# A scan layer's step size summed by TensorE, with its two PSUM banks held as one tile

## The chip, the cores and the metric

The kernel runs on one core of one Trainium2 chip. The metric is the time of one execution in microseconds (us) of device time. Before the change the median of three runs is 3457.79 us (3455.21 to 3458.74). A profiled execution of the same kernel gives the trace that all rows below come from.

The core has five instruction streams that run beside each other and wait for one another by semaphores: PE (TensorE, matrix products, which write into PSUM), DVE (VectorE), ACT (ScalarE), POOL (GpSimd) and SP, which here only issues DMAs. Each stream is strictly in order: an instruction that waits holds up everything behind it on its engine.

## What is computed

The network has four layers on an input of 3 x 256 x 48 x 48 in fp32: a block with attention, a convolution with mixed kernels, a plain convolution, and a selective scan ("layer 3"). Only the scan layer is touched. Cut to what matters, with x the group-normalised input as a sequence of L = 2304 tokens for each of 3 images:

```python
xn  = layernorm(x)                                   # 256 channels
u   = silu(conv1d(xn @ in_proj_w[:512], 4 taps))     # 512 channels
z   = xn @ in_proj_w[512:]
dt_raw, B, C = split(u @ x_proj_w, (16, 16, 16))
dt  = softplus(dt_raw @ dt_proj_w + dt_proj_b)       # 512 channels
for t in range(L):
    h = h * exp(dt[t] * A) + dt[t] * B[t] * u[t]     # 512 x 16 states
    y[t] = sum_n h * C[t]
out = ((y + u * D) * silu(z)) @ out_proj_w
```

The change concerns the line with softplus. In both kernels it is computed as max(v, 0) + ln(1 + exp(-|v|)), where v is what stands in PSUM after the product with dt_proj_w.

## The kernel before

**Tiles.** The 3 x 2304 tokens are worked through in 18 chunks of 384 (CH). The 512 channels are four groups of 128 partitions (m = 0 to 3). For one chunk and one m the 16 states of 128 channels are handled in two steps (h = 0, 1), so a chunk has eight steps; a step has eight parts, one scan each.

**One step.** `fill` (L1711 on DVE, L1715 on POOL) writes dt\*u\*B for the step into the tile hs. `decay` (L1740, ACT) writes exp(dt\*A) for one part into one of three PSUM slots `ps_da`; the decay for part n+3 is issued right after the scan of part n. `scan` (L1748, DVE) runs the recurrence of one part. After the eight parts `times_c` (L1765, POOL) multiplies by C, `add_states` (L1782, PE) sums the states into `ps_y`, and three steps later `gate` (L1789, DVE) reads `ps_y`. `spread_pe` (L1689, PE) copies rows of dt\*u into `ps_r` for the fill two steps ahead. `spread` (L1681) reads dt and dt\*u back from DRAM by DMA, rearranged, for the decays and POOL's fills.

**The preparation.** While one chunk is scanned, the next one's u, B, C, dt and z are made, and the layer norm of the chunk after that. All of it goes through two PSUM banks, `bank[0]` and `bank[1]` (L1206), each a tile of its own, that every stage uses in turn: `less_mean` and `centre` (layer norm), `square_mean`, `inverse_root`, `normalise`; `taps` and `take_u` (u); `project_u` and `take_dbc` (B, C and dt_raw); `project_dt`, `softplus`, `take_dt`, `keep_dt` (dt, two groups at a time: m0 = 0, then 2); `project_z` and `take_z`; `project_y` and `store` (the layer's output).

**The order.** It is written by hand. `plan`, `after` and `gating` (L1373 to L1420) list the stages with a half step j = 0 to 15 and a place in it. `run` (L1422) issues them from the loop of L1800: MID behind the decay of the second of four parts, DONE behind the third, LATE behind the fourth; PE_ at the end of the half step. `keep_order` (L1849) then fixes, for PE, DVE, ACT and POOL, the order in which the instructions were written. So a stage of the preparation stands in the same queue between two decays or two scans. Semaphores are placed automatically, tile by tile, from what each instruction reads and writes.

Chunk 0 is prepared earlier, in `early_preparation` (L1428), while the plain convolution still runs; there each `yield` hands over to the convolution's next group of products. 17 chunks are prepared inside the scan stage, 16 of them with their layer norm.

Of the kernel before, what the change touches and what calls it, by code (L numbers as in the profile page):

```python
# [9 lines left out]
F32 = mybir.dt.float32  # L10
I32 = mybir.dt.int32
AF = mybir.ActivationFunctionType
ALU = mybir.AluOpType
# [3 lines left out]
P = 128  # L17
# [3 lines left out]
CT = 2  # L21
# [4 lines left out]
CH = 384  # L26
# [57 lines left out]
def net(  # L84
# [21 lines left out]
    nc = tc.nc  # L106
# [18 lines left out]
    ident = const.tile([P, P], F32, name="ident")  # L125
# [254 lines left out]
    with ExitStack() as l0:  # L380
# [36 lines left out]
        with ExitStack() as p1:  # L417
# [15 lines left out]
            for b in ORDER:  # L433
# [23 lines left out]
                for c in range(NCH):  # L457
                    for m, dst in ((0, y1), (1, cur[b])):
                        pm = ps.tile([P, 512], F32, tag="s", name="ps_y")
                        for ct in range(CT):  # L460
                            nc.tensor.matmul(  # L461
                                pm[:, :CH], ws[:, ct, m * P : (m + 1) * P], chunk(xb[:, ct, :], c),
                                start=ct == 0, stop=ct == CT - 1,
# [48 lines left out]
        def hidden(b, c):  # L512
            wf, fb = mlp[b]
            f = fpool.tile([P, 2, CH], F32, name="f")
            pf = pair()
            for m in range(2):
                nc.tensor.matmul(
                    pf[:, m, :CH], wf[:, m * P : (m + 1) * P], chunk(cur[b], c),
                    start=True, stop=True,
                )  # L520
            for m in range(2):
                nc.scalar.activation(f[:, m, :], pf[:, m, :CH], AF.Gelu, bias=fb[:, m : m + 1])
            return f
# [10 lines left out]
        with ExitStack() as p2:  # L534
# [9 lines left out]
            for i in range(NB):  # L544
# [400 lines left out]
                for mt in range(0, NT, 2):  # L945
                    pv = pair()
                    for j in range(2):
                        nc.tensor.matmul(
                            pv[:, j, :384], cur[2][:, (mt + j) * P : (mt + j + 1) * P], wn[2],
                            start=True, stop=True,  # L950
# [21 lines left out]
                if i + 1 < NB:  # L972
# [4 lines left out]
                    for b in ORDER:  # L977
                        for c in range(NCH):
                            f = hidden(b, c)
# [84 lines left out]
        for n, b in enumerate(ORDER):  # L1064
            held = None
            for c in range(NCH):
                f = hidden(b, c)
# [38 lines left out]
    psg = ctx.enter_context(tc.tile_pool(name="psg", bufs=1, space=PSUM))  # L1106
    rooms, w3v, chunks, stored = {}, {}, {}, set()

    def room(k, name):
        return rooms[name][k.at % len(rooms[name])]  # L1110
# [47 lines left out]
    def x2_rooms():  # L1158

        block = xpools[2].tile([P, CT, N], F32, name="x2").rearrange("p a b -> p (a b)")  # L1160

        winx, cwb = (t for _, t in divide(
            block, ("winx", P, (CT, DI * P)), ("cwb", P, (DCONV, DI * P))
        ))
        nc.sync.dma_start(winx, w3x.rearrange("(t p) n -> p t n", p=P))
        for k in range(DCONV):
            nc.sync.dma_start(cwb[:, k, :], convw[k : k + 1, :].broadcast_to([P, DI * P]))
        for name, t in divide(
            block, ("u", P, (DI, CH)), ("dtu", P, (DI, CH)), ("dt", P, (DI, CH))
        ):  # L1170
            rooms[name] = [t]
        return winx, cwb

    def fold_taps(winx, cwb, k):
        nc.vector.tensor_tensor(
            w3v["wtap"][:, k, :, :], winx,
            cwb[:, k, :].unsqueeze(1).broadcast_to([P, CT, DI * P]), ALU.mult,
        )
# [15 lines left out]
    def fetch(at):  # L1194
        k = chunks[at] = Chunk()
        k.at = at
        k.b, k.c = todo[at]
        k.before = chunks.get(at - 1)
        k.xg = room(k, "xg")
        nc.sync.dma_start(k.xg, xd[k.b][:, :, k.c * CH : (k.c + 1) * CH])  # L1200
# [2 lines left out]
        pass  # L1203


    bank = [psg.tile([P, 512], F32, name=f"ps_g{j}")[:, :CH] for j in range(2)]  # L1206

    def group_scale(k):  # L1210
        sc, sh = norm3[k.b]
        for ct in range(CT):
            nc.scalar.activation(
                k.xg[:, ct, :], k.xg[:, ct, :], AF.Identity,
                bias=sh[:, ct : ct + 1], scale=sc[:, ct : ct + 1],
            )

    def less_mean(k):

        for to in range(CT):  # L1220
            for ct in range(CT):
                nc.tensor.matmul(  # L1222
                    bank[to], w3v["less"][:, int(to != ct), :], k.xg[:, ct, :],
                    start=ct == 0, stop=ct == CT - 1,
                )

    def square_mean(k):
        for ct in range(CT):
            nc.tensor.matmul(
                bank[1], mean2, k.sq[:, ct, :], start=ct == 0, stop=ct == CT - 1  # L1230
            )

    def centre(k):
        for ct in range(CT):
            nc.scalar.copy(k.xg[:, ct, :], bank[ct])
        k.sq = room(k, "sq")
        nc.scalar.activation(k.sq, k.xg, AF.Square)

    def inverse_root(k):
        var = bank[1]  # L1240
        nc.scalar.activation(var, var, AF.Ln, bias=epst)
        nc.scalar.activation(var, var, AF.Exp, scale=-0.5)

    def normalise(k):
        rs = bank[1].unsqueeze(1).broadcast_to([P, CT, CH])
        nc.vector.tensor_tensor(k.xg, k.xg, rs, ALU.mult)
# [23 lines left out]
    def take_u(k, m):  # L1270
        if m == 0:
            k.u = room(k, "u")
        nc.scalar.activation(
            k.u[:, m, :], bank[m % 2], AF.Identity, bias=v("conv_b", m)
        )
# [31 lines left out]
    def project_dt(k, m0):  # L1307
        for j in range(2):
            m = m0 + j
            nc.tensor.matmul(  # L1310
                bank[j], w3v["dtsb"][:, m * P : (m + 1) * P], k.dbc[: DTR + 1, :],
                start=True, stop=True,
            )

    def softplus(k, m0):

        both = k.dt[:, m0 : m0 + 2, :]
        for j in range(2):
            nc.scalar.activation(k.dt[:, m0 + j, :], bank[j], AF.Abs)
        nc.scalar.activation(both, both, AF.Exp, scale=-1.0)  # L1320
        nc.scalar.activation(both, both, AF.Ln, bias=1.0)

    def take_dt(k, m0):
        for j in range(2):
            m, pdt = m0 + j, bank[j]
            nc.vector.scalar_tensor_tensor(pdt, pdt, 0.0, k.dt[:, m, :], ALU.max, ALU.add)
            nc.vector.tensor_tensor(k.dtu[:, m, :], pdt, k.u[:, m, :], ALU.mult)

    def keep_dt(k, m0):
        for j in range(2):  # L1330
            nc.scalar.copy(k.dt[:, m0 + j, :], bank[j])  # L1331
        if m0 == 0:
            k.dtd, k.dtud = {}, {}
        d = k.dtd[m0] = dram.tile([P, 2, CH], F32, name=f"dtd{m0}")
        nc.sync.dma_start(d, k.dt[:, m0 : m0 + 2, :])
        d = k.dtud[m0] = dram.tile([P // 2, 2, CH], F32, name=f"dtud{m0}")
        nc.sync.dma_start(d, k.dtu[P // 2 :, m0 : m0 + 2, :])

# [25 lines left out]
    def store(k, mo):  # L1364
# [7 lines left out]
    MID, DONE, LATE, PE_ = range(4)  # L1372
# [17 lines left out]
        (7, PE_, 1, project_u),  # L1390
        (8, LATE, 1, take_dbc),
        (8, PE_, 1, lambda k: project_dt(k, 0)),
        (9, LATE, 1, lambda k: softplus(k, 0)),
        (10, MID, 1, lambda k: take_dt(k, 0)),
        (10, DONE, 1, lambda k: keep_dt(k, 0)),
        (10, PE_, 1, lambda k: project_dt(k, 2)),
        (11, LATE, 1, lambda k: softplus(k, 2)),
        (12, MID, 1, lambda k: take_dt(k, 2)),
        (12, DONE, 1, lambda k: keep_dt(k, 2)),
    ]  # L1400

    after = [
# [25 lines left out]
    def early_preparation():  # L1428

        while (2, 1) not in stored:  # L1430
            yield
        fetch(0)
        winx, cwb = x2_rooms()
        k = chunks[0]
        yield
        while 2 not in norm3:
            yield
        group_scale(k)
        yield
        for tap in (0, 1):  # L1440
            fold_taps(winx, cwb, tap)
        less_mean(k)
        yield
        centre(k)
        yield
        square_mean(k)
        yield
        for tap in (2, 3):
            fold_taps(winx, cwb, tap)
        inverse_root(k)  # L1450
        yield
        normalise(k)
        tokens(k)
        fetch(1)
        yield
        for m in (0, 1):
            taps(k, m, 0, 4)
            yield
        take_u(k, 0)
        take_u(k, 1)  # L1460
        yield
        for m in (2, 3):
            taps(k, m, 0, 4)
            yield
        take_u(k, 2)
        take_u(k, 3)
        nc.scalar.activation(k.u, k.u, AF.Silu)
        yield
        k = chunks[1]
        for stage in (group_scale, less_mean, centre, square_mean, inverse_root, normalise):  # L1470
            stage(k)
            yield
        tokens(k)
        yield

        k = chunks[0]
        while 1 not in norm3 or (1, 1) not in stored:
            yield
        x1_rooms()
        yield  # L1480
        project_u(k)
        yield
        take_dbc(k)
        yield
        for m in (0, 2):
            project_dt(k, m)
            yield
            softplus(k, m)
            yield
            take_dt(k, m)  # L1490
            yield
            keep_dt(k, m)
            yield
        for m in (0, 2):
            for j in range(2):
                project_z(k, m + j, j)
            yield
            for j in range(2):
                take_z(k, m + j, j)
            yield  # L1500
# [155 lines left out]
    with ExitStack() as l3:  # L1656
# [136 lines left out]
        k = chunks[0]  # L1793
# [6 lines left out]
        for s, (at, m, h) in enumerate(steps):  # L1800
            if m == 0 and h == 1 and at + 2 <= last:
                fetch(at + 2)
            for part in range(8):
                j = 4 * m + 2 * h + part // 4
# [31 lines left out]
        k = chunks[last]  # L1836
# [122 lines left out]
```

## Time and profile before

| what | value |
| --- | --- |
| runs, median | 3457.79 us |
| profiled execution | 3459.61 us |
| its span in the trace | 3458.2 us |
| scan stage | from about 2020 us to the end |
| clock granted to TensorE, mean | 0.944 |
| ACT busy, whole span | 2351.8 us |
| POOL busy, whole span | 1430.7 us |

How to read what follows. The page gives the busy time of each engine and the costliest groups (line, engine, operation, out<-in, count; then busy us and mean ns of one; then the idle time ahead of them with what ended it). A window row gives busy us of each engine between two times. A timeline row gives start, length, engine, line, operation and count; several equal instructions in a row are merged, and in square brackets stands the idle time before them with what ended it. The tile name ps_g is the banks of the preparation; x, u, wconv and others are blocks of SBUF that hold several things in turn. An fp32 product of 128x384 shows as two instructions.

### The profile page before, as it was taken

What the parts mean: (1) busy time and instruction counts of PE and PEld (TensorE: products, weight loads), DVE (VectorE), ACT (ScalarE), POOL (GpSimd) and SP (SyncE); (2) the same over time, 40 slices, a digit from 0 to 9 for tenths busy, and PEclk for the clock granted to TensorE, in tenths of its full rate; (3) what the DMA queues carried; (4) which work ended last, traced back from release to release, by engine and by line L of the source; (5) the groups of instructions that cost most, each with busy time, mean ns of one, the idle gap of its engine ahead of it and who ended that gap; (6) DMA issues with size and microseconds to landing.
All of it is one profiled execution on the core that took longest, in us unless ns stands there. A gap on an engine that the chain in (4) does not pass through costs nothing.

```text
span 3458.2 us, 51943 instructions
## 1 busy us (share of the span) xinstructions
PE 3125.3 (90%) x20170; PEld 1499.8 (43%) x20170; DVE 2940.7 (85%) x3234; ACT 2351.8 (68%) x3508; POOL 1430.7 (41%) x385
## 2 busy tenths in 40 slices
PE   7999999999999999879999988888888888888885
PEld 4334343443433335447777743333343443333331
DVE  4799899859899994579965379999999999999998
ACT  3788888748888884422224457777777777777774
POOL 0000000000000001110000059999999999999997
PEclk9999999999999999989999989889999999988987
DMA  4000000010000003746402134445444444444441
GB/s 178 14 8 10 8 10 8 8 42 6 10 6 8 10 8 112 249 170 224 139 21 68 46 97 109 115 100 118 116 105 110 106 107 114 116 117 106 117 111 43
DMA packets 167603, 273.95 MB, mean 79 GB/s; under 512 B 30049, under 2 KB 134561, under 8 KB 165426
## 3 DMA queue, kind: packets, MB, share of 16 engines
q1 hardware_dynamic: 154114, 250.48, 26.9%
q10 hardware_dynamic: 13232, 20.06, 1.8%
q8 instruction: 160, 2.62, 0.3%
q14 instruction: 97, 0.79, 0.1%
HBM read 223.12 MB, written 47.10 MB: 78 GB/s over the span
## 4 chain that ended last, share of the span: by engine, by line
PE 54%; DVE 32%; ACT 8%; DMA 3%; issue 2%; POOL 0%; SPq 0%; DVEq 0%; ACTq 0%; POOLq 0%
DVE hs L1748 21%; PE ps_s L637 16%; PE acc L650 14%; PE ps_c L1513 8%; DVE hs L1711 4%; PE ps_g L1222 2%; PE ps_s L1030 2%; ACT ps_da L1740 2%; PE ps_y L461 2%; PE ps_m L664 1%; DVE u L295 1%; PE ps_m L710 1%; ACT L1278 1%; ACT L228 1%; PE acc L528 1%
## 5 line engine op out<-in xcount | busy, mean ns | idle before, releaser
L1748 DVE TENSOR_TENSOR_SCAN hs<-ps_da,hs 128x385 f32<-128x385 f32 x1152 | 1005.6, 938 | 54.4 <-ACT ps_da L1740 35.6
L641 ACT ACTIVATE pt<-ps_s 128x1024 f32<-128x1024 f32 x972 | 942.4, 1022 | 154.8 <-PE ps_s L637 142.2
L856 DVE TENSOR_TENSOR part<-part,pt 128x2048 f32<-128x2048 f32 x396 | 906.6, 2289 | 41.3 <-ACT pt L641 18.5
L1740 ACT ACTIVATE ps_da<-dtr,u 128x384 f32<-128x384 f32 x1152 | 656.0, 582 | 271.3 <-DVE hs L1748 248.4
L163 POOL TENSOR_TENSOR rstd<-ve,mhalf 128x2 f32<-128x2 f32 (+1 forms) x26 | 16.3, 629 | 1477.0 <-DVE ve L161 1477.0
L637 PE MATMUL ps_s<-q,kt 32*128 32x512 f32 (+1 forms) x4320 | 576.4, 592 | 0.1
L650 PE MATMUL acc<-pt,vt 128*32 128x512 f32 (+1 forms) x4320 | 520.9, 561 | 0.2
L1765 POOL TENSOR_TENSOR hc<-hs,x 128x3072 f32<-128x3072 f32 x72 | 446.3, 6198 | 19.8 <-DVE hs L1748 16.5
L1513 PE MATMUL ps_c<-vt,u 128*128 128x288 f32 x1728 | 433.9, 412 | 21.0 <-DVE u L262 21.0
L1765 POOL TENSOR_TENSOR hc<-hs,bc 128x3072 f32<-128x3072 f32 x71 | 438.8, 6181 | 18.6 <-DVE hs L1748 17.2
L1264 PE MATMUL ps_g<-u 128*128 128x384 f32 x1152 | 387.7, 491 | 8.2 <-ACT sz L1349 3.5
L1513 PEld LDWEIGHTS ps_c<-vt,u 128*128 128x128 f32 x1728 | 331.8, 193 | 117.8 <-issue 19.3
L1264 PEld LDWEIGHTS ps_g<-u 128*128 128x128 f32 x1152 | 214.4, 190 | 180.6 <-ACT ps_da L1740 18.7
L637 PEld LDWEIGHTS ps_s<-q,kt 32*128 32x128 f32 x4320 | 195.3, 183 | 199.1 <-issue 120.2
L1782 PE MATMUL ps_y<-hc,u 128*32 128x384 f32 x2304 | 244.8, 548 | 13.8 <-POOL hc L1765 13.8
L1715 POOL TENSOR_TENSOR hs<-dtur,x 128x1536 f32<-128x1536 f32 x72 | 248.4, 3450 | 6.9 <-DMA dtur<-dtud 6.9
L1715 POOL TENSOR_TENSOR hs<-dtur,bc 128x1536 f32<-128x1536 f32 x72 | 249.5, 3465 | 0.0
L650 PEld LDWEIGHTS acc<-pt,vt 128*32 128x32 f32 x4320 | 94.4, 108 | 353.4 <-issue 326.7
L1310 PE MATMUL ps_g<-wconv,u 17*128 17x384 f32 x144 | 79.2, 684 | 82.8 <-ACT x L1331 82.8
L1782 PEld LDWEIGHTS ps_y<-hc,u 128*32 128x32 f32 x2304 | 64.4, 117 | 172.4 <-issue 151.6
L321 POOL MEMSET xpad<- 128x212 f32 x12 | 5.6, 468 | 313.0 <-ACT xpad L1564 234.5
L1529 ACT COPY cb<-ps_c 128x288 f32<-128x288 f32 x48 | 19.2, 400 | 162.9 <-PE ps_c L1513 145.1
(246 smaller groups left out, 3685.3 us busy)
## 6 DMA issues: line engine op xcount, KB each, us to landing
wconv<-in_we SPq DMA_DIRECT2D x144, 384.0 KB, 4.3
dtr<-dtd SPq DMA_DIRECT2D x288, 192.0 KB, 3.9
dtur<-dtud SPq DMA_DIRECT2D x288, 96.0 KB, 4.2
wconv<-xd SPq DMA_DIRECT2D x36, 384.0 KB, 4.3
x<-bcd SPq DMA_DIRECT2D x72, 192.0 KB, 5.7
dtd<-x SPq DMA_DIRECT2D x36, 384.0 KB, 2.9
bc<-bcd SPq DMA_DIRECT2D x72, 192.0 KB, 6.1
yc<-ycat ACTq DMA_DIRECT2D x18, 576.0 KB, 5.0
```

The source lines that it names most:

```text
L637: nc.tensor.matmul(s[:, j, cols], kt[r, mt * P : (mt + 1) * P], q[r, :n], start=True, stop=True,)
L641: nc.scalar.activation(p[:, h0 : h0 + 2, :], s, AF.Exp)
L650: nc.tensor.matmul(acc[h * HD : (h + 1) * HD, :n], vt[:, mt, g * P + h * HD : g * P + (h + 1) * HD], p[:, h, cols], start=mt == 0, stop=mt ...
L856: ): nc.vector.tensor_tensor(part, first, p, ALU.add)
L1264: nc.tensor.matmul(bank[m % 2], w3v["wtap"][:, tap, ct, m * P : (m + 1) * P], k.xn[:, ct, tap : tap + CH], start=tap == 0 and ct == 0, sto ...
L1513: nc.tensor.matmul(pc[:, :HN], u[:, i, dy, ct, m * P : (m + 1) * P], vt[:, i, ct, dy * TW : dy * TW + HN], start=ct == 0 and dy == 0, stop ...
L1711: nc.vector.tensor_tensor(hs[:, :, 0:2, 1:], k.ps[:, :, :CH].unsqueeze(1).broadcast_to([P, 2, 2, CH]), bb, ALU.mult,)
L1715: nc.gpsimd.tensor_tensor(hs[:, :, 2:4, 1:], k.rows[m][1].unsqueeze(1).broadcast_to([P, 2, 2, CH]), bb, ALU.mult,)
L1740: nc.scalar.activation(slots[n % 3][:, 1 : CH + 1], chunks[at].rows[m][0][:, q, :], AF.Exp, scale=amat[:, col : col + 1],)
L1748: nc.vector.tensor_tensor_scan(b, slots[(8 * s + part) % 3][:, : CH + 1], b, 0.0, ALU.mult, ALU.add)
L1765: nc.gpsimd.tensor_tensor(hc, tiles[s][:, :, :, 1:], cb.broadcast_to([P, 2, 4, CH]), ALU.mult)
L1782: nc.tensor.matmul(k.y_ps[32 * q : 32 * q + 32, :CH], fold, hc[:, g, q, :], start=False, stop=h == 1 and g == 1,)
```

## The change

The two banks become one tile of two banks, and both are read by one instruction wherever that is possible (`centre`, the new `positive_part`, `take_dt`, `keep_dt`). max(v, 0) and |v| are taken by ScalarE straight from PSUM; max(v, 0) goes to the room of the other pair of groups (`pair_of(k, 2 - m0)`). After Exp and Ln, TensorE adds the two parts in PSUM by products with the identity matrix (`sum_dt`). VectorE then only multiplies by u.

```diff
-    bank = [psg.tile([P, 512], F32, name=f"ps_g{j}")[:, :CH] for j in range(2)]
+    banks = psg.tile([P, 2, 512], F32, name="ps_g")[:, :, :CH]
+    bank = [banks[:, j, :] for j in range(2)]
...
     def centre(k):
-        for ct in range(CT):
-            nc.scalar.copy(k.xg[:, ct, :], bank[ct])
+        nc.scalar.copy(k.xg, banks)
...
+    def pair_of(k, m0):
+        return k.dt[:, m0 : m0 + 2, :]
+
+    def positive_part(k, m0):
+        nc.scalar.activation(pair_of(k, m0), banks, AF.Abs)
+        nc.scalar.activation(pair_of(k, 2 - m0), banks, AF.Relu)
+
     def softplus(k, m0):
-        both = k.dt[:, m0 : m0 + 2, :]
-        for j in range(2):
-            nc.scalar.activation(k.dt[:, m0 + j, :], bank[j], AF.Abs)
+        both = pair_of(k, m0)
         nc.scalar.activation(both, both, AF.Exp, scale=-1.0)
         nc.scalar.activation(both, both, AF.Ln, bias=1.0)
 
+    def sum_dt(k, m0):
+        for part in (2 - m0, m0):
+            for j in range(2):
+                nc.tensor.matmul(
+                    bank[j], ident, k.dt[:, part + j, :],
+                    start=part != m0, stop=part == m0,
+                )
+
     def take_dt(k, m0):
-        for j in range(2):
-            m, pdt = m0 + j, bank[j]
-            nc.vector.scalar_tensor_tensor(pdt, pdt, 0.0, k.dt[:, m, :], ALU.max, ALU.add)
-            nc.vector.tensor_tensor(k.dtu[:, m, :], pdt, k.u[:, m, :], ALU.mult)
+        nc.vector.tensor_tensor(
+            k.dtu[:, m0 : m0 + 2, :], banks, k.u[:, m0 : m0 + 2, :], ALU.mult
+        )
 
     def keep_dt(k, m0):
-        for j in range(2):
-            nc.scalar.copy(k.dt[:, m0 + j, :], bank[j])
+        nc.scalar.copy(pair_of(k, m0), banks)
...
+        (9, MID, 1, lambda k: positive_part(k, 0)),
         (9, LATE, 1, lambda k: softplus(k, 0)),
-        (10, MID, 1, lambda k: take_dt(k, 0)),
-        (10, DONE, 1, lambda k: keep_dt(k, 0)),
+        (9, PE_, 1, lambda k: sum_dt(k, 0)),
+        (10, DONE, 1, lambda k: take_dt(k, 0)),
+        (10, LATE, 1, lambda k: keep_dt(k, 0)),
         (10, PE_, 1, lambda k: project_dt(k, 2)),
+        (11, MID, 1, lambda k: positive_part(k, 2)),
         (11, LATE, 1, lambda k: softplus(k, 2)),
-        (12, MID, 1, lambda k: take_dt(k, 2)),
-        (12, DONE, 1, lambda k: keep_dt(k, 2)),
+        (11, PE_, 1, lambda k: sum_dt(k, 2)),
+        (12, DONE, 1, lambda k: take_dt(k, 2)),
+        (12, LATE, 1, lambda k: keep_dt(k, 2)),
```

In `early_preparation` the same stages are called in the same order, with one more `yield` for each pair.

The built programs also differ in the semaphores that stages wait for whose lines the diff does not touch. Read from the two programs, for one chunk:

| stage (engine, place) | before it waits for | after it waits for |
| --- | --- | --- |
| take_u(0) (ACT, 2 MID) | last product of taps(0), bank 0 | last product of taps(1), bank 1 |
| take_u(2) (ACT, 5 MID) | last product of taps(2) | last product of taps(3) |
| take_u(3) (ACT, 6 MID) | last product of taps(3) | last product of project_y(0) |
| store(1) (ACT, 8 MID) | last product of project_y(1) | last product of project_u |
| inverse_root, Ln (ACT, 14 MID) | last product of square_mean | last product of project_z(0) |
| normalise (DVE, 15 MID) | no product | last product of project_z(1) |
| take_z(1) (ACT, 15 MID) | last product of project_z(1) | normalise on DVE |
| taps(0) (PE, 0 PE_) | take_z(2) | take_z(3) |
| taps(2) (PE, 3 PE_) | take_u(0) | take_u(1) |
| project_y(0) (PE, 5 PE_) | take_u(2) | take_u(2) |
| positive_part(2), Relu (ACT, 11 MID) | (no such stage) | the DMA that stores dt of the first pair |

More of the change, by code (lines that the diff above doesn't have):

```diff
@@ L1334, in keep_dt @@
         d = k.dtd[m0] = dram.tile([P, 2, CH], F32, name=f"dtd{m0}")
-        nc.sync.dma_start(d, k.dt[:, m0 : m0 + 2, :])
+        nc.sync.dma_start(d, pair_of(k, m0))
         d = k.dtud[m0] = dram.tile([P // 2, 2, CH], F32, name=f"dtud{m0}")
@@ L1487, in early_preparation @@
             yield
+            positive_part(k, m)
             softplus(k, m)
+            yield
+            sum_dt(k, m)
             yield
```

## The prediction

> **What bounds the kernel now.** I read the page's busy times first, then the costliest groups, then the busy times of one chunk of the scan stage, then the four timelines of that chunk.
>
> ```profile
> PE 3125.3 (90%) x20170; PEld 1499.8 (43%) x20170; DVE 2940.7 (85%) x3234; ACT 2351.8 (68%) x3508; POOL 1430.7 (41%) x385
> ...
> L1748 DVE TENSOR_TENSOR_SCAN hs<-ps_da,hs 128x385 f32<-128x385 f32 x1152 | 1005.6, 938 | 54.4 <-ACT ps_da L1740 35.6
> ```
> PE's 90% is an average over other stages. All that the change touches lies behind about 2020 us, where the scans run.
>
> ```profile
> 2411.20:2489.30 78.10, 66.49 (x280) 30.68 (x280) 75.61 (x86) 60.83 (x113) 76.24 (x18) 0.90 0.47 112
> ```
> The columns are window, length, then PE, PEld, DVE, ACT and POOL busy. In one chunk DVE works 75.6 of 78.1 us. POOL, at 76.2, is as full.
>
> ```profile
> 2435.46 6.91 DVE L1748 TENSOR_TENSOR_SCAN hs<-ps_da,hs 128x385 f32<-128x385 f32 x8
> ...
> 2453.82 6.91 DVE L1748 TENSOR_TENSOR_SCAN hs<-ps_da,hs 128x385 f32<-128x385 f32 x8
> ...
> 2472.19 1.81 DVE L1748 TENSOR_TENSOR_SCAN hs<-ps_da,hs 128x385 f32<-128x385 f32 x2
> 2473.92 0.54 DVE L1326 SCALAR_TENSOR_TENSOR ps_g<-ps_g,x 128x384 f32<-128x384 f32 x1
> 2474.49 0.56 DVE L1327 TENSOR_TENSOR x<-ps_g,x 128x384 f32<-128x384 f32 x1
> 2474.97 0.56 DVE L1326 SCALAR_TENSOR_TENSOR ps_g<-ps_g,x 128x384 f32<-128x384 f32 x1
> 2475.56 0.56 DVE L1327 TENSOR_TENSOR x<-ps_g,x 128x384 f32<-128x384 f32 x1
> 2476.03 5.20 DVE L1748 TENSOR_TENSOR_SCAN hs<-ps_da,hs 128x385 f32<-128x385 f32 x6
> ```
> DVE's timeline has hardly a gap (three of 0.47 to 0.58 us in this chunk). So DVE's chain is the end of the stage: a scan starts every 6.91/8 = 0.864 us, and take_dt's four instructions take 2476.03-2473.92 = 2.11 us. POOL runs steps of 9.55 us back to back through most of the chunk (fills start at 2440.43, 2449.99, 2459.52), so it allows 8 x 9.55 = 76.4 us a chunk. DVE's chunk is 78.6 on average (2174.86 to 3196.33 in the chain of waits, 13 chunks). So DVE may win 2.2 us a chunk, no more; what it loses shows in full.
>
> **What the change removes.** In each of 17 chunks, twice, 2.11 us of DVE give way to one 128x768 multiply with a PSUM operand. Nearest row: normalise (L1246), 128x768 with ps_g, takes 0.93 and starts its successor 0.85 later; half a fill (L1711, 128x1536) is 0.87. So 0.86, bounds 0.85 and 1.0: 1.25 won each time, **2.5 us a chunk**.
>
> **What it adds.** (1) TensorE: 8 products of 128x384 in fp32 a chunk, 0.68 us each (L1355, eight instructions for four products, 2.74): 5.5 on 66.5 busy of 78: no bound by itself. (2) ScalarE: ten 384-wide reads of PSUM (0.475) go, seven 768-wide come (0.844, the Exp and Ln rows): 1.2 us more on 60.8, no bound either. ACT rows with one table set show no reload between Exp, Abs and Ln; I take Relu as free of one too. (3) Waits. Both banks are now one tile, and the two built programs differ in what each reader waits for (listed under the change): an instruction on one bank now waits for the last user of either. ScalarE is in order, and behind the waiting instruction stand the decays (L1740) that each scan needs. Decays are three parts ahead of the scans, so a hold costs DVE what exceeds that lead.
>
> I walk the chunk along the rows of before, each time with earlier stalls already added to both sides; hops between engines cost 0.05 (copy's end to L1222's start).
>
> ```profile
> 2429.16 0.85 ACT L1349 COPY sz<-ps_g 128x384 f32<-128x384 f32 x2
> ...
> 2437.82 0.56 ACT L1273 ACTIVATE x<-ps_g,vec 128x384 f32<-128x384 f32 x1
> 2438.28 1.30 ACT L1740 ACTIVATE ps_da<-dtr,u 128x384 f32<-128x384 f32 x2
> ...
> 2450.93 0.56 ACT L1273 ACTIVATE x<-ps_g,vec 128x384 f32<-128x384 f32 x1
> ```
> ```profile
> 2429.78 10.56 PE L1264 MATMUL ps_g<-u 128*128 128x384 f32 x32 [0.51 <-ACT sz L1349]
> ...
> 2449.97 5.43 PE L1264 MATMUL ps_g<-u 128*128 128x384 f32 x16
> ...
> 2478.07 2.92 PE L1310 MATMUL ps_g<-wconv,u 17*128 17x384 f32 x4 [4.92 <-ACT x L1331]
> ```
>
> A. take_u(0) ran at 2437.82, in the midst of PE's taps. Now it waits for taps(1), which end at 2440.34, and 0.38 later because they wait for both take_z copies. It starts at 2440.77, the next decay 0.46 later, ended at 2441.8. That decay serves part 5 of step 1, due at 2435.46+5x0.864 = 2439.78. **Stall 2.1**, from 1.7 (no later start) to 3.
>
> B. take_u(2) (2450.93) now waits for taps(3). taps(2) waits for take_u(1), 2.1 late: 2443.93; then 5.26, the ps_y work 2.17, taps(3) 5.27 (differences of PE starts): 2456.63. Next decay ends 2457.72; part 1 of step 3 is due at 2453.82+0.86+2.1 = 2456.78. **1.0**, from 0.5 (the 0.47 stall of step 2 absorbs it) to 2.
>
> C. take_u(3) waits for project_y(0), which starts only after take_u(2) (2457.29) and needs 3.31: 2460.6. Next decay ends 2461.69, due 2457.77+4x0.864 = 2461.23. **0.5**, from 0 to 1. D. store(1) waits for project_u, 0.6 after its slot, with 0.37 of lead: **0.25**, from 0 to 0.6.
>
> E. project_dt(0) ends at 2470.58. Abs and Relu (0.78 apart), two decays (0.52), Exp (0.88) and Ln (0.84) end at 2474.96. The last two products of sum_dt take 1.37: 2476.4. take_dt, after three scans, is due at 2472.19+2.59 = 2474.78. **1.65**, from 0.8 (Ln a decay earlier) to 2. Behind sum_dt on PE stand the ps_y products (1.43) and spread_pe (0.85); they end near 2478.7, and gate and fill, which read them, are due after 2481: hidden.
>
> F. take_dt and one scan later (2478.16), a decay, then keep_dt's copy, over at 2479.57. project_dt(2) waits for it and takes 2.93 at the slow clock, to 2482.55; Relu also overwrites what the DMA of dtd0 reads (2.9 to landing, 2482.5). ScalarE stands still there for 1.7 us; Abs, Relu and the next decay end at 2484.8. Meanwhile DVE does four scans, gate (0.45) and fill (1.84) and one scan more, due at 2484.77: **0.1**, without the gate and fill 2.4. dtd0 lands 1.2 later than before and is read by spread some 2 us after that, for decays 10 us later still: hidden.
>
> G. One more decay, Exp and Ln end at 2486.95, two products at 2488.35; take_dt is due two scans after 2484.85, at 2486.58: **1.8**, from 1.0 to 2.4.
>
> H. less_mean starts one scan later, as keep_dt moved from DONE to LATE (2412.05 for 2411.19). inverse_root's Ln now waits for project_z(0): at full clock 2.72 for less_mean, copy and Square, 1.4 for square_mean and 1.38 for project_z give 2419.45 for the Ln that ran at 2418.77. Ln, Exp and take_z (0.58+0.47+0.37) put the decay of part 5 at 2421.5, due 2420.43: 1.1, of which 0.58 stands there already, so 0.5. Then normalise on DVE, due 2422.4, waits for project_z(1) (2422.22 to 2423.8): 1.4. With less_mean at its present 4.54, the first rises to 2.2 and hides the second. **2.1**, from 0.5 to 2.5.
>
> Clock: after 4.92 us of idleness L1310's four took 2.92; at 2469.03, after none, 1.55. The waits before these become about 1 to 2 us each; I charge the slow clock in F and half of it in H. (The Trainium skill, "TensorE: Matmul & The Clock Gate", section "What's actually happening", says that a window of about 3.4 us without work halves the clock; by it the shorter pauses keep the clock, and by my estimate from its rule the sum would lose about 0.2 us a chunk.)
>
> At A the row speaks for itself: ScalarE reads one bank at 2437.82 while PE is writing the other until 2440.34. (The Trainium skill, "PSUM — Partial Sum Buffer", section "PSUM bank collisions raise a hardware error", states that only users of the same bank and quadrant of partitions collide. By it none of the waits of A to D and H is needed, and without them the sum would be near +1.05 us a chunk; but the program issues its waits whether or not the memory needs them.)
>
> **Sum.** 2.1+1.0+0.5+0.25+1.65+0.1+1.8+2.1 = 9.5, less 2.5: **+7.0 us a chunk**; x17 = 119, less 2.1 as the norm stage (H) runs in 16: 117. POOL then waits more and binds nothing. At the end of the convolution stage (PE full, 27.0 of 27 us in 1990 to 2017) chunk 0's sum_dt adds 8 x 0.69 = 5.5 us of PE, between nothing (the first scan waits for dtr, landed 2025.67) and 11 (PE also waiting for Ln): +5. The profiled execution took 3459.61 (span 3458.2, 1.4 around it), 1.8 over the median of the runs. 3459.6+122 = 3581.6, less 1.8: **3580 us.**
>
> **Rivals.**
> 1. *The lead of the decays hides all holds* (faster, 3%). Three slots, gate and fill cover a hold at F; if they did so at every place, DVE gains 2.5 and POOL stops it at 2.2: 3457.8-17x2.2 = 3420. It decides if the eight stalls sum to less than 2.5 us. Against it: A alone holds ScalarE 3 us with 0.92 of lead.
> 2. *Only the longer path to dt costs* (7%), so E, F and G remain: 3.55-2.5 = +1.05 a chunk, +18, +5: 3481. For it: ScalarE idles 17 us a chunk. Against it: the waits stand in the built program.
> 3. *More is late* (12%): slow clock at each new pause (8 products at twice 0.68 instead of once) puts up to 1.4 us each on E and G: near +9.5 a chunk, 3625 to 3640.
> The forecast has 78%, with +4 to +9 a chunk: 3525 to 3620. The range takes in most of rival 3 and the lower bounds of E, G and H: **3515 to 3635.** A measurement of this kernel tells about 0.2% from no change. Faster 0.03, within it 0.01, slower 0.96.
>
> **What would show it.** Right: chunks of 85 to 86 us; DVE's scans waiting on decays at step 1 part 5 and step 3 part 1, and take_dt waiting for sum_dt by 1.5 to 2; take_u(0) ending ScalarE's idleness on L1264's last product; POOL idle 8 us a chunk. Wrong: chunks under 80 us (the holds are hidden), or a stall at a place not listed.

## The result and the profile after

The changed kernel takes 3573.44 us in the median of four runs (3572.78 to 3576.57), against 3458.26 us for the kernel before: ratio 1.0335, 95% interval 1.0317 to 1.0353. It is slower by 115 us. The forecast was 3580 us.

The profiled execution took 3572.99 us, 113.4 more than that of before. Two lines of its page, the busy times and the costliest group, answer to the first two shown above.

```profile
PE 3191.7 (89%) x20458; PEld 1538.9 (43%) x20458; DVE 2910.5 (81%) x3126; ACT 2357.5 (66%) x3454; POOL 1433.8 (40%) x385
...
L1768 DVE TENSOR_TENSOR_SCAN hs<-ps_da,hs 128x385 f32<-128x385 f32 x1152 | 1012.8, 940 | 126.4 <-ACT ps_da L1760 109.0 <-POOL hs L1735 1.6
```

DVE is busy for 30 us less, and the scans have waited 109.0 us for decays where it was 35.6. No engine has become full. The line numbers have moved: the scan is now L1768, the decay L1760, sum_dt L1333, take_dt L1339.

The busy times of 15 whole chunks, from the first taps of one chunk to those of the 15th after it, before:

```profile
2115.01:3293.17 1178.16, 1002.90 (x4201) 461.91 (x4201) 1134.58 (x1276) 921.04 (x1768) 1146.00 (x243) 0.90 0.46 111
```

and after:

```profile
2119.82:3400.07 1280.25, 1061.21 (x4441) 495.44 (x4441) 1110.12 (x1186) 925.71 (x1723) 1149.31 (x243) 0.95 0.42 102
```

A chunk went from 78.54 to 85.35 us. DVE's own work (third busy column) fell by 24.5 us, and its idle time rose from 43.6 to 170.1 us. So +8.43 us of standing less 1.63 us of work is the +6.8 us a chunk. The granted clock rose from 0.90 to 0.95, so TensorE was not slower on the whole; at single places it was (see the last section).

DVE's timeline of one chunk after, its rows that end a stall (the time in brackets, and what ended it):

```profile
2984.77 2.66 DVE L1768 TENSOR_TENSOR_SCAN hs<-ps_da,hs 128x385 f32<-128x385 f32 x3 [2.02 <-ACT ps_da L1760]
...
3000.89 3.51 DVE L1768 TENSOR_TENSOR_SCAN hs<-ps_da,hs 128x385 f32<-128x385 f32 x4 [1.04 <-ACT ps_da L1760]
3005.06 2.66 DVE L1768 TENSOR_TENSOR_SCAN hs<-ps_da,hs 128x385 f32<-128x385 f32 x3 [0.66 <-ACT ps_da L1760]
...
3015.04 2.66 DVE L1768 TENSOR_TENSOR_SCAN hs<-ps_da,hs 128x385 f32<-128x385 f32 x3 [0.17 <-ACT ps_da L1760]
...
3023.42 0.96 DVE L1339 TENSOR_TENSOR x<-ps_g,x 128x768 f32<-128x768 f32 x1 [1.30 <-PE ps_g L1333]
...
3035.46 0.96 DVE L1339 TENSOR_TENSOR x<-ps_g,x 128x768 f32<-128x768 f32 x1 [1.95 <-PE ps_g L1333]
...
3048.27 0.96 DVE L1768 TENSOR_TENSOR_SCAN hs<-ps_da,hs 128x385 f32<-128x385 f32 x1 [1.48 <-ACT ps_da L1760]
3049.94 0.95 DVE L1246 TENSOR_TENSOR wconv<-wconv,ps_g 128x768 f32<-128x768 f32 x1 [0.71 <-PE ps_g L1354]
```

These are the stalls A, B, C, D, E, G and the two of H, in this order. ScalarE's rows of the same chunk show what is behind the first two:

```profile
2983.69 0.58 ACT L1273 ACTIVATE x<-ps_g,vec 128x384 f32<-128x384 f32 x1 [2.86 <-PE ps_g L1264]
...
2999.80 0.58 ACT L1273 ACTIVATE x<-ps_g,vec 128x384 f32<-128x384 f32 x1 [3.75 <-PE ps_g L1264]
```

take_u(0) and take_u(2) stand for 2.86 and 3.75 us until TensorE has written the *other* bank, and the decays stand in the queue behind them.

### The profile page after: what moved, and what is told of

It reads as the page before. It is cut to its first block, busy times and chain, and to the rows that moved or that the text cites. A ratio compares the mean times of both kernels' runs of the same rounds, so it can differ in the third digit from the quotient of the medians.

```text
span 3571.3 us, 52385 instructions
## 1 busy us (share of the span) xinstructions
PE 3191.7 (89%) x20458; PEld 1538.9 (43%) x20458; DVE 2910.5 (81%) x3126; ACT 2357.5 (66%) x3454; POOL 1433.8 (40%) x385
## 4 chain that ended last, share of the span: by engine, by line
PE 71%; DVE 13%; ACT 10%; issue 3%; DMA 2%; POOL 0%; SPq 0%; ACTq 0%; DVEq 0%; POOLq 0%
PE ps_s L637 15%; PE acc L650 13%; PE ps_g L1264 11%; PE ps_c L1533 8%; DVE hs L1768 6%; PE ps_g L1333 4%; ACT ps_da L1760 3%; PE ps_y L1802 2%; DVE u L295 2%; PE ps_g L1284 1%; PE ps_y L461 1%; PE ps_s L1030 1%; PE ps_m L664 1%; PE ps_g L1223 1%; PE ps_g L1310 1%
## 5 line engine op out<-in xcount | busy, mean ns | idle before, releaser
L1768 DVE TENSOR_TENSOR_SCAN hs<-ps_da,hs 128x385 f32<-128x385 f32 x1152 | 1012.8, 940 | 126.4 <-ACT ps_da L1760 109.0
L1760 ACT ACTIVATE ps_da<-dtr,u 128x384 f32<-128x384 f32 x1152 | 647.5, 580 | 219.1 <-DVE hs L1768 208.3
L1264 PE MATMUL ps_g<-u 128*128 128x384 f32 x1152 | 387.9, 492 | 49.7 <-ACT x L1362 14.6
L1802 PE MATMUL ps_y<-hc,u 128*32 128x384 f32 x2304 | 223.2, 506 | 13.5 <-POOL hc L1785 13.5
L1333 PE MATMUL ps_g<-x,ident 128*128 128x384 f32 x288 | 156.6, 697 | 73.5 <-ACT x L1321 58.7
L1333 PEld LDWEIGHTS ps_g<-x,ident 128*128 128x128 f32 x288 | 68.5, 262 | 155.4 <-ACT x L1321 80.3
L1354 PE MATMUL ps_g<-u 128*128 128x384 f32 x288 | 106.7, 503 | 29.1 <-ACT sz L1362 15.0
```

The costliest lines, as they stand in the source:

```text
L1264: nc.tensor.matmul(bank[m % 2], w3v["wtap"][:, tap, ct, m * P : (m + 1) * P], k.xn[:, ct, tap : tap + CH], start=tap == 0 and ct == 0, sto ...
L1333: nc.tensor.matmul(bank[j], ident, k.dt[:, part + j, :], start=part != m0, stop=part == m0,)
L1760: nc.scalar.activation(slots[n % 3][:, 1 : CH + 1], chunks[at].rows[m][0][:, q, :], AF.Exp, scale=amat[:, col : col + 1],)
L1768: nc.vector.tensor_tensor_scan(b, slots[(8 * s + part) % 3][:, : CH + 1], b, 0.0, ALU.mult, ALU.add)
L1802: nc.tensor.matmul(k.y_ps[32 * q : 32 * q + 32, :CH], fold, hc[:, g, q, :], start=False, stop=h == 1 and g == 1,)
```

## The experiments

**Theory:** most of the loss comes from the two banks being one tile, by waits on a bank that the instruction does not touch; the sum by TensorE costs little by itself. **Rival:** the longer path to dt (Abs, Relu, Exp, Ln and then sum_dt before take_dt) is the cost, whatever the tiles.

**1. The change with two tiles.** Each bank is a tile again; Abs, Relu, the multiply and the copies go by bank. The sum stays on TensorE.

```diff
-    banks = psg.tile([P, 2, 512], F32, name="ps_g")[:, :, :CH]
-    bank = [banks[:, j, :] for j in range(2)]
+    bank = [psg.tile([P, 512], F32, name=f"ps_g{j}")[:, :CH] for j in range(2)]
...
-        nc.vector.tensor_tensor(
-            k.dtu[:, m0 : m0 + 2, :], banks, k.u[:, m0 : m0 + 2, :], ALU.mult
-        )
+        for j in range(2):
+            nc.vector.tensor_tensor(k.dtu[:, m0 + j, :], bank[j], k.u[:, m0 + j, :], ALU.mult)
...
```

> The changed kernel with the two banks as two tiles again; whatever read both in one instruction does it in two (Abs, Relu, copies, the multiply). Theory (the waits between the banks, stalls A to D, H and normalise, measured 5.5 us a chunk in the changed kernel): these go, the late take_dt (1.3 and 1.95) stays, DVE pays 0.07 us more a multiply: 3573 - 17x5.5 + 2 = 3482. Rival (the longer path to dt is what costs, and the other waits only move with it): within 10 us of 3573.

Measured: 3465.93 us, ratio to before 1.0026 (1.0015 to 1.0037): +10 us against the runs of before beside it, where the changed kernel had +115. The expectation was 16 us too high. What remains at take_dt, from DVE's timeline of one chunk:

```profile
2954.66 1.20 DVE L1342 TENSOR_TENSOR x<-ps_g,x 128x384 f32<-128x384 f32 x2 [0.63 <-PE ps_g L1335]
...
2965.95 0.56 DVE L1342 TENSOR_TENSOR x<-ps_g,x 128x384 f32<-128x384 f32 x1 [0.94 <-PE ps_g L1335]
2967.23 0.56 DVE L1342 TENSOR_TENSOR x<-ps_g,x 128x384 f32<-128x384 f32 x1 [0.72 <-PE ps_g L1335]
```

DVE stands 0.63 + 0.94 + 0.72 = 2.29 us for sum_dt, about what it saves. (The Trainium skill, "PSUM — Partial Sum Buffer", section "PSUM bank collisions raise a hardware error", says that only users of one bank and quadrant collide; this run agrees: take_u(0) reads one bank at 2917.01 us while TensorE's taps write the other until 2919.52, and none of the waits A to D and H is needed.)

**2. The tile alone.** The kernel before, with nothing but the allocation changed.

```diff
-    bank = [psg.tile([P, 512], F32, name=f"ps_g{j}")[:, :CH] for j in range(2)]
+    banks = psg.tile([P, 2, 512], F32, name="ps_g")[:, :, :CH]
+    bank = [banks[:, j, :] for j in range(2)]
```

> The kernel before with nothing but the allocation changed: one tile of two banks, all instructions as before. Theory: A to D, H and normalise appear without any change of work: 3458 + 17x5.5 = 3552, chunks of 84 us. Rival (the longer path costs): 3458, chunks of 78.6.

Measured: 3569.70 us, ratio 1.0330 (1.0312 to 1.0348): not an instruction more or less, and nearly the whole loss. It is 18 us more than expected: its chunks took 85.36 us and not 84, those of the changed kernel 85.35. DVE's timeline shows the same places:

```profile
2983.11 2.66 DVE L1749 TENSOR_TENSOR_SCAN hs<-ps_da,hs 128x385 f32<-128x385 f32 x3 [2.02 <-ACT ps_da L1741]
...
2999.23 3.51 DVE L1749 TENSOR_TENSOR_SCAN hs<-ps_da,hs 128x385 f32<-128x385 f32 x4 [1.04 <-ACT ps_da L1741]
...
3046.89 0.96 DVE L1749 TENSOR_TENSOR_SCAN hs<-ps_da,hs 128x385 f32<-128x385 f32 x1 [2.44 <-ACT ps_da L1741]
```

The first two stalls are those of the changed kernel to the hundredth; the last is 0.96 us longer (less_mean takes 4.54 us here, as before, and 2.85 in the changed kernel). The rival is out: the path to dt is that of before here, and the time is not. The two together (+114 alone, +115 with the rest, each against the runs of before beside it) also show that the other parts nearly cancel.

**3 and 4. take_dt later, reading dt from SBUF.** To give sum_dt more time, take_dt was put one half step later, behind keep_dt, with dt read from keep_dt's copy in SBUF; once with one tile (3), once with two (4). Relu goes to the room of dt\*u.

```diff
-            k.dtu[:, m0 : m0 + 2, :], banks, k.u[:, m0 : m0 + 2, :], ALU.mult
+            k.dtu[:, m0 : m0 + 2, :], pair_of(k, m0), k.u[:, m0 : m0 + 2, :], ALU.mult
...
-        (10, DONE, 1, lambda k: take_dt(k, 0)),
+        (11, DONE, 1, lambda k: take_dt(k, 0)),
...
```

> The changed kernel, one tile kept, but take_dt reads dt from SBUF after keep_dt and stands two and a half steps' parts later (half steps 11 and 13), Relu goes to the room of dtu. Theory: VectorE no longer waits for sum_dt, so the two stalls of 1.3 and 1.95 us go and the rest stays: 3573 - 17x3.25 = 3518. Rival (the wait moves to ScalarE, where keep_dt now holds the decays instead): within 10 us of 3573.

> Two tiles and the late take_dt together. Theory: no stall is left of those found, VectorE keeps what the change saves (2.3 us a chunk), up to GpSimd's bound of 76.4 us a chunk: 3458 - 17x2.2 = 3421, up to 3435 if some is lost to ScalarE's 1.7 us more a chunk. Rival (what was saved on VectorE is lost again to ScalarE or GpSimd): 3450 or more.

Measured: 3594.53 us with one tile (1.0401, 1.0383 to 1.0418) and 3513.45 us with two (1.0158, 1.0135 to 1.0181). Both missed: slower than the kernels they came from. The waits for sum_dt were gone as meant. But the multiply itself had grown; DVE's timeline of the run with two tiles:

```profile
2983.99 4.43 DVE L1341 TENSOR_TENSOR x<-x 128x768 f32<-128x768 f32 x1
...
2997.49 2.36 DVE L1341 TENSOR_TENSOR x<-x 128x768 f32<-128x768 f32 x1
```

and GpSimd's at the same time:

```profile
2984.15 3.46 POOL L1738 TENSOR_TENSOR hs<-dtur,bc 128x1536 f32<-128x1536 f32 x1
...
2995.60 3.44 POOL L1738 TENSOR_TENSOR hs<-dtur,bc 128x1536 f32<-128x1536 f32 x1
```

The same multiply took 0.96 us with an operand in PSUM. Now each ended 0.8 us after a fill of GpSimd (2987.61 and 2999.04): as if it had run only then. Up to here that is an argument; the next run tests it.

**5. One operand from SBUF, and nothing else.** The kernel before, with one operand exchanged; dt\*u then leaves out the positive part.

```diff
-            nc.vector.tensor_tensor(k.dtu[:, m, :], pdt, k.u[:, m, :], ALU.mult)
+            nc.vector.tensor_tensor(k.dtu[:, m, :], k.dt[:, m, :], k.u[:, m, :], ALU.mult)
```

> The kernel before, with one operand of take_dt's multiply exchanged: it reads the logarithm's part from SBUF and not the sum from PSUM (so the positive part is left out of dt*u); count, shapes and places are those of before. Theory: a DVE instruction whose two operands both lie in SBUF does not run beside GpSimd's fill and times_c, and waits for the end of the one running: in the run with the late multiply from SBUF it took 3.05 to 3.17 us on average where 0.95 is usual, +2.2; four a chunk, 17 chunks: +150, 3608 us (3530 to 3700), and the four multiplies show 1.5 to 4 us instead of 0.56. Rival: the long multiplies of that run came from something of its own (order, semaphores): 3458 here, multiplies at 0.56.

Measured: 3650.92 us, ratio 1.0554 (1.0537 to 1.0570), +193 where +150 was expected. In the scan stage the multiplies took 3.48 and 3.52 us on average for 0.56. DVE:

```profile
2978.66 7.90 DVE L1327 TENSOR_TENSOR dtu<-x,u 128x384 f32<-128x384 f32 x1
...
2986.96 0.54 DVE L1327 TENSOR_TENSOR dtu<-x,u 128x384 f32<-128x384 f32 x1
```

GpSimd:

```profile
2976.57 6.21 POOL L1765 TENSOR_TENSOR hc<-hs,x 128x3072 f32<-128x3072 f32 x1
2982.69 3.47 POOL L1715 TENSOR_TENSOR hs<-dtur,x 128x1536 f32<-128x1536 f32 x1
2992.79 6.20 POOL L1765 TENSOR_TENSOR hc<-hs,x 128x3072 f32<-128x3072 f32 x1 [6.64 <-DVE hs L1748]
```

The first multiply waits out two instructions of GpSimd and ends 0.40 us after the second (2986.16). The next one, at 2986.96, finds GpSimd idle and takes 0.54. That settles runs 3 and 4. (The Trainium skill, "SBUF — State Buffer", section "Who interferes with whom", says that a VectorE instruction with two inputs in SBUF contends with a GpSimd instruction that reads SBUF, over a shared port pair that is an exclusive lock. These rows agree for VectorE, which waits to the end of GpSimd's instruction and finishes 0.40 us after it.)

**6. take_dt one scan later, still from PSUM.** Run 1 with DONE changed to LATE for both take_dt.

> The changed kernel with two tiles again, and take_dt one scan later (LATE in place of DONE). Theory: with the false waits gone, what is left of the cost is DVE standing before take_dt for sum_dt, 19.6+17.6 us over 15 or 16 chunks in the run with two tiles; one scan more in front (0.87 us) takes away up to 0.87 of each: 3466-17x2x0.85 = 3437, below the kernel before (3458). Rival: the wait moves on to project_dt(2) and less_mean, which need the bank free, and comes back at the next decays: 3466, no gain.

Measured: 3443.37 us, ratio 0.9965 (0.9951 to 0.9979): 0.35% faster than before, little but clear of its interval, and 6 us over the expectation. DVE's wait for sum_dt fell from 42.7 us in run 1 to 14.1 in the whole execution. Part of what was left came from another wait, in ScalarE's timeline:

```profile
2938.38 0.87 ACT L1323 ACTIVATE x<-ps_g 128x384 f32<-128x384 f32 x2 [1.53 <-DMA dtd<-x]
```

Relu of the second pair overwrites dt of the first, and waits until the DMA has stored it; in the first chunk of the stage ScalarE waited 7.97 us for it, and DVE behind it 5.96.

**7. Relu into the room of dt\*u.** Run 6 with that wait taken away by another place for the positive part.

```diff
+    def positive(k, m0):
+        return (k.dtu if m0 else k.dt)[:, 2:4, :]
...
-            nc.scalar.activation(k.dt[:, 2 - m0 + j, :], bank[j], AF.Relu)
+            nc.scalar.activation(positive(k, m0)[:, j, :], bank[j], AF.Relu)
...
```

> Two tiles with the late take_dt, and the positive part of the second pair goes to the room of dt*u and not to that of dt's first pair, so its Relu no longer waits for the DMA that stores dt (1.53 us of ScalarE in the run before, and behind it 0.54+0.27+0.51 = 1.32 us of DVE standing for a decay and for sum_dt). Theory: that wait is their cause; the chunk falls from 77.35 to what GpSimd allows, 76.4: 3443-17x0.95 = 3427. Rival: ScalarE would only wait for DVE in its place, the 1.32 us stay: 3443.

Measured: 3427.54 us, ratio 0.9922 (0.9907 to 0.9938): the fastest kernel of this study that computes the whole layer. The time is as expected (beside it, before took 3453.95), for two reasons and not one: the chunk fell from 77.35 to 76.76 us (9 us in 15 chunks), and the stall of about 6 us in the first chunk is gone. Its 15 chunks:

```profile
2111.31:3262.65 1151.34, 1046.16 (x4440) 492.60 (x4441) 1102.72 (x1216) 940.09 (x1828) 1145.42 (x243) 0.96 0.47 113
```

GpSimd is busy for 1145 of 1151 us: now it is the bound.

**8. No take_dt at all.** What is DVE's time worth, if none of it is paid back?

```diff
-        k.dtu = room(k, "dtu")
+        k.dtu = k.u
...
     def take_dt(k, m0):
-        for j in range(2):
-            m, pdt = m0 + j, bank[j]
-            nc.vector.scalar_tensor_tensor(pdt, pdt, 0.0, k.dt[:, m, :], ALU.max, ALU.add)
-            nc.vector.tensor_tensor(k.dtu[:, m, :], pdt, k.u[:, m, :], ALU.mult)
+        pass
...
-            nc.scalar.copy(k.dt[:, m0 + j, :], bank[j])
+            nc.scalar.activation(k.dt[:, m0 + j, :], bank[j], AF.Abs)
```

This kernel leaves out the sum and the multiply: |v| stands for dt, and u for dt\*u.

> The kernel before without take_dt: DVE's four instructions a pair are left out (dt is |v|, dt*u is u), the rest stands. It asks what DVE's time is worth when none of it is paid back in waits. Theory (GpSimd's eight steps of 9.55 us are the next bound): the chunk falls from 78.6 to 76.4 only, 3458-17x2.2 = 3420. Rival (no such bound): all 4.2 us a chunk are won, 3458-17x4.2 = 3386.

Measured: 3418.04 us, ratio 0.9884 (0.9869 to 0.9899). Eight steps of it:

```profile
2905.67:2981.87 76.20, 68.15 (x282) 31.35 (x281) 71.86 (x78) 61.14 (x115) 76.20 (x17) 0.89 0.48 115
```

GpSimd never rests, and the chunk stops at 76.2 us although DVE has only 71.9 us of work. The bound of rival 1 (3420 us) is real; run 7 comes within 10 us of it.

**9 and 10. One term at a time, with one tile.** In the changed kernel, take_u(0) one half step later (9), and take_dt one scan later (10).

```diff
-        (2, MID, 1, lambda k: take_u(k, 0)),
+        (3, MID, 1, lambda k: take_u(k, 0)),
```

> The changed kernel (one tile) with take_u(0) one half step later, beside take_u(1), so that taps(1) is long over when ScalarE comes to it. Theory: stall A (2.02 us a chunk) goes and the others stay: 3573-17x2.0 = 3539. Rival: the stalls share one slack, and what A gives up B and C take: 3573, no change.

> The changed kernel (one tile) with take_dt one scan later alone. Theory: stalls E and G (1.30 and 1.95 us) each lose the 0.87 us of one scan and nothing comes back: 3573-17x1.74 = 3543. Rival: as with take_u(0), two thirds come back at other places, since PE and ScalarE stand in each other's way all through the chunk: 3573-17x0.6 = 3563.

Measured: 3562.96 us (1.0301, 1.0285 to 1.0317) and 3562.95 us (1.0310, 1.0290 to 1.0331). Each is 10 us below the changed kernel, where its theory said 34 and 30. Against the runs of before beside it, run 10 wins only 6, and its interval overlaps that of the changed kernel. The rival of (10), 3563 us, was right; that of (9), no change, was nearer than its theory. In (9) stall A is gone, but take_u(0) now delays what is behind it, and B grows from 1.04 to 1.87 us:

```profile
2991.48 3.51 DVE L1768 TENSOR_TENSOR_SCAN hs<-ps_da,hs 128x385 f32<-128x385 f32 x4 [1.87 <-ACT ps_da L1760]
```

Over the whole execution the waits for decays fell from 109.0 to 90.2 us, and those for sum_dt rose from 60.1 to 65.8. In (10) the waits for sum_dt fell from 60.1 to 41.5 us, those for decays rose by 7. One reason is the clock: in the chunk shown of the changed kernel the four products that end sum_dt(0) took 1.56 us, here 2.93. They ran slow in 14 of the 17 chunks here, and in five there; over the execution one product instruction of sum_dt took 767 ns on average for 697.

```profile
3020.48 2.05 PE L1333 MATMUL ps_g<-x,ident 128*128 128x384 f32 x4 [1.60 <-ACT x L1321]
3023.09 2.93 PE L1333 MATMUL ps_g<-x,ident 128*128 128x384 f32 x4 [0.56 <-ACT x L1327]
```

## Why the prediction held, point by point

| step | forecast, us a chunk | in the chunk shown |
| --- | --- | --- |
| saving at take_dt | -2.5 | -2.47 |
| A, take_u(0) | 2.1 | 2.02 |
| B, take_u(2) | 1.0 | 1.04 |
| C, take_u(3) | 0.5 | 0.66 |
| D, store(1) | 0.25 | 0.17 |
| E, take_dt(0) | 1.65 | 1.30 |
| F, project_dt(2) | 0.1 | 0 |
| G, take_dt(2) | 1.8 | 1.95 |
| H, Ln and normalise | 2.1 | 1.61 (1.48 less the 0.58 of before, and 0.71) |
| sum | +7.0 | +6.28; mean of 15 chunks +6.81 |

- **The bound** was read rightly: DVE's chain ends the stage, and what it loses shows in full. Run 8 confirms the other side, GpSimd at 76.2 us a chunk.
- **The saving** is as worked out: the multiply takes 0.96 us and its successor starts 0.87 after it, against 2.11. ScalarE's added work, put at 1.2 us a chunk, was 0.3 (925.71 less 921.04 over 15 chunks); it bound nothing either way.
- **A to D** hold to 0.16 us, and run 2 shows that they belong to the tile alone: 2.02, 1.04, 0.66 and 0.17 there as well.
- **E and H** are smaller in the chunk shown. In H, L1223 (less_mean) kept the full clock (2.85 us for eight; before, 4.54), which had been charged by half. In run 2, where less_mean is slow, the stall of normalise stays 0.71 beside the 2.44: the first does not hide the second, where the forecast said that it would. E was 1.30 or 1.31 in eleven of the 17 chunks and 2.67 or 2.68 in the five where sum_dt(0) ran slow; its mean is 1.74, that of G 1.79. **F** is hidden, as said.
- **The 0.53 us** by which the mean exceeds the chunk's sum were not in the forecast. A part of it is probably the breaks: a scan with its successor ready gives way after 0.864 us, the last one before a stall lasts 0.96, and there are six to eight more such breaks. This agrees with DVE's busy time, which fell by 1.63 us a chunk and not by 2.47; run 2 supports it, where DVE with the same instructions as before is busy for 12.7 us more (2953.4), 0.75 a chunk. No run varies the breaks alone.
- **The end of the convolution stage** was mis-sized: +5 us was forecast, and the first scan started at 2028.13 for 2027.58. 17 x 6.81 less the norm's one chunk is 114, and the whole difference was 113.4: nothing is left for that term. In the kernels with two tiles the first scan started between 2022.0 and 2033.6 us, and in run 2, with the instructions of before, at 2023.4, which none of the edits explains; what sets it stays open.
- **The clock** was charged at other places than where it fell, and that G came out right is partly luck. From the start of take_dt(0) to the end of the second Ln the forecast had 10.5 us and the chunk shown has 9.0, as project_dt(2), charged with 2.93 us in F, ran in 1.55. But the products behind that Ln, forecast at 1.4 us, ran slow and took 3.0 (all eight of the pair 5.54). The two errors nearly cancel.
- **Rival 1** failed where the prediction said: A alone exceeds the lead of the decays. Its price was right. **Rival 2** (E, F and G alone, 3481 us) did not happen, but run 1 is its case: 3466 us. A chunk of run 1 takes 78.28 us, 0.26 less than before, where the rival had +1.05; what it loses it loses once, at the stage's start (first scan 6.0 us later) and in the first chunk (6.09 us, Relu's wait for the DMA of dt, which F had put down as hidden; in the changed kernel itself no such stall shows). **Rival 3** took the slow clock to fall at both sums in each chunk; where it fell at G, as in the chunk shown, the stall was 1.95, and where it fell at E 2.67, but it did not fall fully on both.

## What to carry to other kernels

Before two buffers are merged into one tile to save an instruction, list who waits for whom in the built program: here the merge alone cost 114 us, with no instruction changed, because in-order queues carried each false wait to the scans. Here the moved operation paid only once its consumer stood later: one scan's distance and another place for one operand turned 3466 into 3428 us, while the same products with one tile cost 3573. Price a stall together with what it holds behind it: taking one of eight away returned a third of its size.

## What the runs showed that was not expected

**VectorE waits out GpSimd's instructions** when its two operands both lie in SBUF: 3.5 us on average for a multiply that takes 0.56 with one operand in PSUM, and GpSimd's times_c keeps its 6.2 us beside the latter. In this kernel DVE's frequent instructions of the scan stage read PSUM for one operand.

**TensorE's clock can fall with no long pause.** Two rows of TensorE in the chunk shown of the changed kernel, and ahead of them one of an earlier chunk:

```profile
2251.03 5.54 PE L1333 MATMUL ps_g<-x,ident 128*128 128x384 f32 x8 [1.60 <-ACT x L1321]
...
3019.21 1.56 PE L1333 MATMUL ps_g<-x,ident 128*128 128x384 f32 x4 [1.60 <-ACT x L1321]
...
3029.88 5.54 PE L1333 MATMUL ps_g<-x,ident 128*128 128x384 f32 x8 [1.69 <-ACT x L1321]
```

In the chunk shown the products ran at full clock after a pause of 1.60 us; after pauses of 0.99 and 1.69 us, with 1.55 us of work between them, they took 0.69 us each, and the granted clock was 0.56 from 3028 to 3032. In the earlier chunk they were slow after the same pause of 1.60 us, so the length of the last pause alone does not decide. Which of the two sums is slow changes from chunk to chunk: the first in five of 17, the second in twelve. (The Trainium skill, "TensorE: Matmul & The Clock Gate", section "What's actually happening", speaks of a window of about 3.4 us without work. No pause in the rows of the chunk shown reached half of that, so these rows do not agree with the rule as the prediction read it, and the measurement decides; what the clock counts was not settled.)
